# A graph layer's gathers paced over one core: one stage per iteration, and more columns fetched by VectorE and ScalarE

## The chip, the cores and the metric

The kernel runs on one core of a Trainium2 chip. The metric is the device time of one execution in microseconds (us); less is better. "The profile" is one execution recorded by the hardware profiler, "the span" the time from its first to its last instruction. The core's engines work side by side, each through its own queue of instructions in order: TensorE (PE, its weight loads PEld) multiplies matrices, VectorE (DVE) and ScalarE (ACT) work element by element, GpSimd (POOL) issues gathers, SyncE (SP) issues the other transfers. They wait for one another through semaphores.

## The reference

The graph has 12,500 nodes of 64 features (`x`) and 200,000 edges (`src`, `dst`), sorted by `dst`. Each edge has 64 features and a distance. What is computed, with `ssp(v) = softplus(v) - log 2`:

```python
nodes = x[edges].reshape(num_edges, -1)              # 128: x[src], x[dst]
gates = ssp(edge_state @ We1 + be1) @ We2 + be2
gates = gates * (1.0 - sigmoid(5.0 * (edges_distance - 3.5)))
h = ssp(nodes @ Wn1 + bn1) @ Wn2 + bn2
messages = h * gates
message_sum = zeros_like(x).at[edges[:, 1]].add(messages)
new = x + (ssp(message_sum @ Ws1 + bs1) @ Ws2 + bs2)
out = layernorm(x + new)
```

All is float32.

## The kernel before

**Tiling.** The edges are cut into 391 groups of 512 (the last is partly padding). A group is four slots of 128 edges; a slot's rows of `x[src]` come to 128 partitions with one indirect transfer that GpSimd issues (`gather`, L195 to L206): four gathers a group, into a tile `xg` of which eight exist. Since the edges are sorted by target, the 256 edges of half a group reach nodes within a window of 42 rows. So the target side of the first node layer, `x[dst] @ Wn1[64:] + bn1`, is computed once per node in 98 chunks of 128 nodes (`chunk`, `keep_chunk`), stored to a table in HBM, and its window is fetched by SP (`load`, L210 to L226). A one-hot matrix (`onehot`) picks each edge's row, and `scatter` with the same matrix sums the messages.

**A group's way.** `gather` and `load`; `onehot` (VectorE) writes the one-hot columns beside the gathered rows in `xg`; `transposes` (TensorE, L281) bring the four slots to feature-major in PSUM, `xcopy` (ScalarE, L289) copies them to SBUF; `layer1_bias`, `layer1_edge` and `layer1_node` (TensorE) make the 768 pre-activations of edge and node side in a PSUM tile `z`; `exps` and `logs` (ScalarE) and `softplus` (VectorE) the activation; `layer2` (TensorE, L354 and L359) both second layers into a PSUM tile `gh`; `hcut` and `message` (VectorE) multiply h, cutoff and gates; `scatter` (TensorE, L376) sums into a spare part of `z`; `window` (VectorE, L396) adds that to `sums`, which holds the sums of all nodes in SBUF. `z`, `gh` and the transposes' tile `tx` exist twice each.

**The loop.** The order of the work is written out by hand; each engine takes its instructions in that order. Iteration i issues the gathers of group i + 3 and the loads of group i + 5, then on TensorE: biases, `scatter` of group i - 2, `transposes` of i + 1, the edge layer of i + 1, a chunk (or, without one, a matmul whose result nobody reads, `busy`), the node layer of i + 1, another `busy`, `layer2` of i. So within an iteration the node layer waits for `xcopy`, which waits for the transposes just before it; `exps`, `logs` and `softplus` of the same group follow, and `layer2` of group i takes the activation that the iteration before made. A gather waits for its tile: the `scatter` of the group eight before it.

**Columns.** Some slots are not gathered. The kernel holds `x` transposed in SBUF (`xh`, two halves of the nodes on 64 partitions each), and VectorE and ScalarE copy 128 single columns of four bytes each into a tile (`columns`, L259), at addresses that they first load into registers from `columns_at` (`read_columns`, L242, one TENSOR_LOAD an iteration and engine). `choose` keeps the half that holds the node, and `layer1_node` multiplies the result by its own weights. VectorE copies 8 columns an iteration and ScalarE 16, which comes to 70 such slots, in groups that lie apart; those groups gather three slots.

**Node blocks.** When `sums` is complete for a block of 512 nodes (25 blocks), `node_block` runs the output layers and the layer norm in eleven steps, spread over later iterations; the steps of the last block follow the loop. The last twelve iterations run in a closer order (`CLOSE`, `behind_by`), with `scatter` one group behind instead of two.

## Time and profile before

| | |
|---|---|
| runs before | 2359.99, 2363.53, 2370.9 us; median 2363.53 |
| the profiled execution | 2389.88 us, span 2388.1, mean granted TensorE clock 0.981 |
| TensorE busy | 1970.5 us (83% of the span) |
| VectorE, ScalarE busy | 1293.9 (54%), 1511.2 (63%) |
| GpSimd busy | 1417.0 (59%), 1493 gathers |
| columns copied by ScalarE, VectorE | 6016 in 608.7 us, 2944 in 246.5 us |

How to read the lines that follow. A row of the page's groups, or of the view by line, names source line, engine, operation, output and inputs and their shapes, the count, then busy us and mean ns of one, then the idle time of the engine just before them and what ended it. Rows in order of time begin with start and length in us; several like instructions in a row are one row (x8), and a bracket gives the idle time before it with what released it. "issue" means that the profile shows nothing that was waited for. Releasers are inferred from semaphore events, and the ends of matmuls are modelled. A row by windows has the stretch, its length, busy us (instructions) of PE, PEld, DVE, ACT and POOL, the granted clock, the DMA engines' busy share and GB/s. Rows of one line alone give shortest, median and longest ns.

### The profile page before, as it was taken

Reading aid. Unit: us, or ns where it says so; the run is one execution under the profiler, and the core shown is the slowest. Engines: PE = TensorE matmul, PEld = TensorE weight load, DVE = VectorE, ACT = ScalarE, POOL = GpSimd, SP = SyncE. Lnnn points to the kernel's source line nnn. Section 1 sums busy time; section 2 is a strip of 40 time slices with the busy share of each in tenths; the row PEclk is TensorE's granted clock in tenths of the full one; section 3 lists DMA queues with packets and bytes.
Section 4 is the critical chain, followed back from the end, with each engine's and each line's share of the span. In section 5 each row is a group of like instructions: output and inputs, shape, how many; then the busy total and the mean of one; then the engine's idle time right before and its main releaser. Section 6 shows DMA issues by size and latency. Waiting matters only on the chain.

```text
span 2388.1 us, 48209 instructions
## 1 busy us (share of the span) xinstructions
PE 1970.5 (83%) x12897; PEld 1656.7 (69%) x12897; DVE 1293.9 (54%) x5966; ACT 1511.2 (63%) x7412; POOL 1417.0 (59%) x1497
## 2 busy tenths in 40 slices
PE   6788888888888888888888888888888888888877
PEld 4666677767776776677677667766777767777765
DVE  4355555555555555555555555555555555555544
ACT  3466666666666666666666666666666666666653
POOL 5665665666666666666666666665665666666650
PEclk9799999999999999999999999999999999999988
DMA  6332232322222222222222222222222222222220
GB/s 185 85 91 68 56 75 56 77 61 71 54 57 56 53 59 54 57 56 62 53 59 55 57 58 55 59 59 54 58 58 56 59 57 60 63 57 58 59 50 14
DMA packets 159679, 148.63 MB, mean 62 GB/s; under 512 B 40564, under 2 KB 108949, under 8 KB 159274
## 3 DMA queue, kind: packets, MB, share of 16 engines
q1 hardware_dynamic: 111194, 94.97, 14.4%
q0 software_dynamic: 47776, 49.02, 10.8%
q8 instruction: 109, 1.79, 0.3%
q14 instruction: 166, 1.36, 0.2%
q10 hardware_dynamic: 434, 1.50, 0.2%
HBM read 135.70 MB, written 9.62 MB: 61 GB/s over the span
## 4 chain that ended last, share of the span: by engine, by line
PE 80%; issue 13%; ACT 3%; DVE 2%; another core or an unknown queue 1%; DMA 0%; DVEq 0%; ACTq 0%
PE z L308 18%; PE gh L359 13%; PE z L376 10%; PE tx L283 10%; PE gh L354 7%; PE z L301 6%; PE gh L334 4%; PE gh L347 3%; PE z L296 3%; PE z L334 2%; ACT xT L291 2%; PE tx L415 1%; PE tx L446 1%; PE z L311 1%
## 5 line engine op out<-in xcount | busy, mean ns | idle before, releaser
L204 POOL DMA_INDIRECT xg<-in_x,src_i x1493 | 1416.8, 949 | 919.3 <-PE tx L283 488.8
L308 PE MATMUL z<-xT,wns 106*128 106x256 f32 x1564 | 459.7, 412 | 359.9 <-issue 285.9
L291 ACT COPY xT<-tx 106x512 f32<-106x512 f32 x391 | 229.1, 586 | 779.3 <-PE tx L283 751.1
L259 ACT COPY column<-xh 128x4 uint8 x6016 | 608.7, 193 | 0.0
L308 PEld LDWEIGHTS z<-xT,wns 106*128 106x128 f32 x1564 | 267.8, 193 | 452.4 <-issue 337.7
L368 DVE TENSOR_TENSOR h<-gh,cut 128x256 f32<-128x256 f32 x391 | 165.9, 424 | 747.9 <-PE tx L283 632.2
L359 PE MATMUL gh<-consts,s 128*128 128x64 f32 x3128 | 396.0, 270 | 0.0
L359 PEld LDWEIGHTS gh<-consts,s 128*128 128x128 f32 x3128 | 385.0, 194 | 0.1
L325 ACT ACTIVATE u<-u,one 128x768 f32<-128x768 f32 x392 | 365.8, 933 | 13.4 <-ACT u L322 0.5
L330 DVE SCALAR_TENSOR_TENSOR s<-u,z 128x768 f32<-128x768 f32 x392 | 368.7, 941 | 0.4 <-issue 0.4
L322 ACT ACTIVATE u<-z 128x768 f32<-128x768 f32 x392 | 314.7, 803 | 43.4 <-PE z L308 19.0
L396 DVE TENSOR_TENSOR sums<-sums,z 64x42 f32 x778 | 152.4, 196 | 291.3 <-issue 207.4
L376 PEld LDWEIGHTS z<-xg,msg 128*128 128x128 f32 x1556 | 205.0, 192 | 140.6 <-issue 121.3
L376 PE MATMUL z<-xg,msg 128*128 128x84 f32 x1556 | 265.1, 293 | 15.3 <-DVE msg L372 15.3
L259 DVE COPY column<-xh 128x4 uint8 x2944 | 246.5, 219 | 0.4 <-issue 0.4
L354 PE MATMUL gh<-consts,s 128*128 128x128 f32 x1564 | 243.3, 279 | 1.3 <-DVE s L330 0.8
L283 PE MATMUL tx<-consts,xg 128*106 128x128 f32 x1564 | 238.1, 276 | 0.0
L301 PE MATMUL z<-eT,consts 128*128 128x256 f32 x782 | 237.3, 386 | 0.0
L354 PEld LDWEIGHTS gh<-consts,s 128*128 128x128 f32 x1564 | 210.0, 195 | 2.0 <-DVE s L330 1.1
L283 PEld LDWEIGHTS tx<-consts,xg 128*106 128x106 f32 x1564 | 182.5, 142 | 0.9 <-issue 0.9
L372 DVE TENSOR_TENSOR msg<-gh,h 128x256 f32<-128x256 f32 x391 | 165.8, 424 | 13.4
L334 PEld LDWEIGHTS gh<-consts 128*128 128x128 f32 x778 | 149.5, 195 | 20.5 <-issue 0.3
(109 smaller groups left out, 1456.2 us busy)
## 6 DMA issues: line engine op xcount, KB each, us to landing
eT<-in_eT SPq DMA_DIRECT2D x195, 256.0 KB
xg<-in_x,src_i POOLq DMA_INDIRECT x1493
wns<-table SPq DMA_DIRECT2D x782, 21.0 KB
table<-tb SPq DMA_DIRECT2D x14, 448.0 KB
side<-in_sides SPq DMA_DIRECT2D x70, 64.0 KB
y<-in_x SPq DMA_DIRECT2D x24, 128.0 KB
out<-y SPq DMA_DIRECT2D x24, 128.0 KB
xh<-in_xh SPq DMA_DIRECT2D x2, 781.5 KB
```

The costliest lines, as they stand in the source:

```text
L204: behind(note(("gather", g), nc.gpsimd.indirect_dma_start(out=xg[:, k, :D], out_offset=None, in_=x, in_offset=bass.IndirectOffsetOnAxis(ap ...
L259: copy(column_tiles[slot].bitcast(U8)[:, 4 * r : 4 * r + 4], xh[:, bass.ds(column_at[queue][j] - xh_at, 4)])
L283: ins = nc.tensor.transpose(tx[:, k, :], xgs[g][:, k, :DW], ident)
L301: nc.tensor.matmul(zs[g][:, 0, :HE], we1.rearrange("a h d -> a (h d)"), eTs[g], start=False, stop=True, skip_group_check=True)
L308: nc.tensor.matmul(zn, wns[:, g % REST, h, :], xTs[g][:, h], start=True, stop=not chosen, skip_group_check=True)
L322: nc.scalar.activation(us[g][:, part], z_of(g)[:, part], AF.Exp)
L325: nc.scalar.activation(us[g][:, part], us[g][:, part], AF.Ln, bias=one)
L330: nc.vector.scalar_tensor_tensor(ss[g].rearrange("p i t e -> p (i t e)")[:, part], us[g][:, part], BIG, z_of(g)[:, part], OP.min, OP.max)
L334: nc.tensor.matmul(z, we1.rearrange("a h d -> a (h d)"), ident, start=True, stop=True, skip_group_check=True)
L354: nc.tensor.matmul(v[:, 0, t], ss[g][:, 0, t, :], we2, start=False, stop=False, skip_group_check=True)
L359: nc.tensor.matmul(ghs[g][:, 1, 2 * t + h, :], ss[g][:, 1 + h, t, :], wn2, start=False, stop=h == 1 and t == 1, skip_group_check=True)
L376: ins = nc.tensor.matmul(sc, msgs[g][:, 2 * t : 2 * t + 2, :].rearrange("p h f -> p (h f)"), xgs[g][:, 2 * t : 2 * t + 2, D:DW], start=t = ...
```

## The change

*Stages.* Every step of a group has an iteration of its own, by a table of lags: group i is transposed in iteration i, copied out in i + 1, has its first layers in i + 2, exponential and logarithm in i + 3, `softplus` in i + 4, `layer2` in i + 5, message in i + 6, `scatter` in i + 7, `window` in i + 9. On TensorE an iteration runs bias, `scatter`, `layer2`, the edge layer, a chunk or part of a node block, the node layer, the transposes. There is no closer order at the end: the loop goes on until all stages are through.

*`keep`.* A new ScalarE copy brings pre-activations, sums and a node block's or chunk's part (852 or 980 elements) from PSUM to SBUF one iteration after TensorE wrote them; `softplus` and `window` read that copy.

*Gates.* A group's first gather waits for the last `layer2` matmul that the iteration before issued and for the transposes of five groups back; there are twelve `xg` tiles. `load` runs three groups ahead and waits for the same transposes.

*Columns.* VectorE copies 28 and ScalarE 18 columns in an iteration whose group i + 3 gathers four slots, else 20 and 10: 120 slots instead of 70. The addresses of VectorE's columns are loaded in two halves, behind `softplus` and behind `message`; ScalarE's behind the logarithm. `choose` runs one iteration after a slot is whole.

*`busy`.* One stands before the transposes and one before the node layer, both only where group i + 3 gathers four slots, the second only where no chunk and no node block uses the place.

*Node blocks* are cut to parts of 128 columns, one TensorE part an iteration, on a copy of their sums; at most as many iterations as their gaps say. *The start* brings the first 8 groups' indices in a transfer of their own, `x` transposed in 14 pieces, and does part of the preparation inside iterations 1 to 4.

The diff, cut to its core:

```diff
+LAGS = dict(xcopy=1, z=2, exps=3, softplus=4, layer2=5, message=6, sums=7, window=9)
+BUFS = AHEAD + LAGS["sums"] + 2
+GATE = AHEAD + 2
+FETCH = 3
-COLUMNS = (8, 16)
+FEW, MANY = (20, 10), (28, 18)
...
+    def count(queue, i, known):
+        return (FEW if i + AHEAD > known or i + AHEAD in taken else MANY)[queue] if i >= COLUMNS_FROM else 0
...
+    def gather(g):
+        xgs[g] = loads.tile([P, K, P], F32, name="xg", bufs=BUFS)
+        xg, needs, n = xgs[g], [("layer2", g - AHEAD - 1 - LAGS["layer2"]), ("transposes", g - GATE)], 0
...
-        old = ("scatter", g - LOADS - 4)
+        old = ("transposes", g - GATE)
...
     def transposes(g, *needs):
-        tx = tx_tile()[:DW].rearrange("f (k e) -> f k e", k=K)
+        tx = tx_tile()
+        if gathered(g + AHEAD) == K:
+            busy(tx[:, :P])
+        tx = tx[:DW].rearrange("f (k e) -> f k e", k=K)
...
+    def keep(z, n, summed, extra):
+        ends = (0, 3 * HE, 3 * HE + 2 * W, 3 * HE + 2 * W + P)
+        held = [n is not None, summed is not None, bool(extra)]
...
+                nc.scalar.copy(c[:, ends[at] : ends[end]], z.rearrange("p b e -> p (b e)")[:, ends[at] : ends[end]])
...
-        nc.vector.scalar_tensor_tensor(ss[g].rearrange("p i t e -> p (i t e)")[:, part], us[g][:, part], BIG,
-                                       z_of(g)[:, part], OP.min, OP.max)
+        nc.vector.scalar_tensor_tensor(ss[g].rearrange("p i t e -> p (i t e)"), us[g], BIG, cs[g], OP.min, OP.max)
...
+            i = -AHEAD
+            while i <= NG + lag["window"] or blocks:
+                zt = z_tile()
+                n = i - lag["z"]
...
+                at(load, i + FETCH)
+                at(gather, i + AHEAD)
+                at(layer1_bias, n, ("load", n))
+                summed = i - lag["sums"]
+                at(scatter, summed, zt[:, 1, HE : HE + 2 * W])
+                at(layer2_bias, i - lag["layer2"])
+                at(layer2, i - lag["layer2"])
+                at(layer1_edge, n)
...
+                if free and 0 <= n < NG and gathered(i + AHEAD) == K:
+                    busy_before_node(n)
+                at(layer1_node, n)
+                at(transposes, i, ("gather", i), ("onehot", i))
+
+                at(xcopy, i - lag["xcopy"])
+                at(exps, i - lag["exps"])
+                extra = keep(*kept)
+                at(logs, i - lag["exps"])
...
+                at(softplus, i - lag["softplus"])
+                read_columns(i, 0, 0, 2)
+                at(hcut, i - lag["message"])
+                at(message, i - lag["message"])
+                read_columns(i, 0, 1, 2)
+                at(onehot, i + 1)
+                at(window, i - lag["window"])
...
+                read_columns(i, 1)
+                for queue in (1, 0):
+                    if 0 <= i < NG:
+                        columns(i, queue, finish)
```

## Prediction

> **What bounds the kernel now.** I read the page first, then the order of time on each engine in the middle of the run, then the chain of waits, then the start and the end.

> ```profile
> span 2388.1 us, 48209 instructions
> L204 POOL DMA_INDIRECT xg<-in_x,src_i x1493 | 1416.8, 949 | 919.3 <-PE tx L283 488.8
> ```

> No engine is full: GpSimd works 1416.8 of 2388.1 us on 1493 gathers and stands idle 919.3. GpSimd alone, in order of time (start, length, idle time before it):

> ```profile
> 1203.69 0.94 POOL L204 DMA_INDIRECT xg<-in_x,src_i  x1 [1.41 <-PE tx L283]
> 1204.94 0.95 POOL L204 DMA_INDIRECT xg<-in_x,src_i  x1 [0.30 <-issue]
> ...
> 1207.44 0.94 POOL L204 DMA_INDIRECT xg<-in_x,src_i  x1 [0.30 <-issue]
> 1209.87 0.94 POOL L204 DMA_INDIRECT xg<-in_x,src_i  x1 [1.49 <-PE tx L283]
> ...
> 1212.37 0.94 POOL L204 DMA_INDIRECT xg<-in_x,src_i  x1 [0.30 <-issue]
> 1214.66 0.94 POOL L204 DMA_INDIRECT xg<-in_x,src_i  x1 [1.35 <-PE tx L283]
> ```

> A group's gathers form a burst, 1.25 us apart. From burst to burst it takes 6.18 us with four gathers (1203.69 to 1209.87) and 4.79 with three (1209.87 to 1214.66). Between bursts lie 2.43 and 2.29 us instead of 1.25. Why, show the other engines in the same stretch:

> ```profile
> 1205.29 0.66 DVE L259 COPY column<-xh 128x4 uint8 x8
> 1205.79 1.00 PE L359 MATMUL gh<-consts,s 128*128 128x64 f32 x8
> 1207.66 0.60 PE L283 MATMUL tx<-consts,xg 128*106 128x128 f32 x4
> 1209.56 0.42 DVE L368 TENSOR_TENSOR h<-gh,cut 128x256 f32<-128x256 f32 x1 [2.79 <-PE tx L283]
> 1209.69 0.59 ACT L291 COPY xT<-tx 106x512 f32<-106x512 f32 x1 [2.40 <-PE tx L283]
> 1211.70 0.81 ACT L322 ACTIVATE u<-z 128x768 f32<-128x768 f32 x1
> ```

> TensorE ends layer two (L359) at 1206.79 and the transposes (L283) at 1208.26, by its records. Yet VectorE's `hcut`, which needs only L359, starts at 1209.56, ScalarE's `xcopy` at 1209.69, and the next gather, which waits for `scatter` between the two, at 1209.87: all within 0.31 us, and 2.1 us after the last gather of the burst was issued (1207.44). In the three-gather burst the last is issued at 1212.37 and the next burst opens 2.29 us later. At the end, where no gather is left:

> ```profile
> 2346.39 1.00 PE L359 MATMUL gh<-consts,s 128*128 128x64 f32 x8
> 2347.43 0.42 DVE L368 TENSOR_TENSOR h<-gh,cut 128x256 f32<-128x256 f32 x1 [0.26 <-PE gh L359]
> ```

> There `hcut` follows L359 by 0.04 us. So I read: late in a burst TensorE's completions reach nobody until the burst's last gather has landed, some 2.1 us after its issue. Early in a burst they do: L322 starts at 1211.70, right behind the L308 matmuls (below: 1210.33 + 1.13 = 1211.46), 1.8 us into the burst of 1209.87. The chain of waits (start, us, what) shows what TensorE would need by itself:

> ```profile
> 1210.33 1.13 PE z L308 x4
> ...
> 1211.69 0.45 PE gh L354 x4
> 1212.13 0.84 PE gh L359 x8
> 1212.97 0.21 PE z L296
> 1213.18 0.22 PE gh L347
> 1213.40 0.60 PE z L376 x4
> ...
> 1215.10 0.03 issue
> 1215.12 1.13 PE z L308 x4
> ```

> 4.79 us from L308 to L308, of which it waits 0.03: 4.76 of work, against 6.18 a four-gather iteration takes. The bound is the burst, its landing and the wait that opens the next one. From group 11 to group 390 there are 379 such intervals, 70 of them behind three gathers:

> ```profile
> 78.08 0.94 POOL L204 DMA_INDIRECT xg<-in_x,src_i  x1 [3.51 <-remote]
> 2332.80 0.94 POOL L204 DMA_INDIRECT xg<-in_x,src_i  x1 [3.01 <-PE z L376]
> ```

> 309 × 6.18 + 70 × 4.79 = 2245 us; between the two rows lie 2254.7.

> **The change, part by part.** *Fewer gathers.* Written out, the new plan gives 120 groups of three gathers (75 by VectorE, 45 by ScalarE) for 70: fifty intervals shrink by 1.39, 69.5 us. The 50 more side loads (64 KB each) go to SP's queue, none lies in GpSimd's.

> *Engine time for it.* Of the same 102 iterations (us, then busy time of PE, PEld, DVE, ACT, POOL):

> ```profile
> 1000.00:1600.00 600.00, 502.01 (x3352) 423.00 (x3352) 330.39 (x1554) 393.10 (x1966) 368.01 (x389) 1.00 0.24 57
> L259 ACT COPY column<-xh 128x4 uint8 x1628 | 164.7, 193 | 0.0
> L259 DVE COPY column<-xh 128x4 uint8 x808 | 67.0, 221 | 0.0
> L291 ACT COPY xT<-tx 106x512 f32<-106x512 f32 x102 | 59.8, 586 | 199.5 <-PE tx L283 199.5
> L322 ACT ACTIVATE u<-z 128x768 f32<-128x768 f32 x102 | 82.0, 804 | 0.0
> ```

> VectorE: (330.39 - 67.0) / 102 = 2.58 us beside the columns, a column 67.0 / 808 = 0.083; with 28 it has 4.90 us, with 20 4.24. ScalarE: (393.10 - 164.7) / 102 = 2.24, a column 0.101, and `keep`, a new copy of 852 elements out of PSUM in every iteration. Its price lies between 0.80 (L322, 768 elements) and 0.98 (L291's 586 ns scaled by 852/512); I take 0.9. That is 4.96 with 18 columns and 4.15 with 10. All stay under 6.18 and 4.79, so they hide in the idle time that the burst leaves; without that cover a four-gather iteration could not go under 4.96.

> *Address loads.* They run on the sequencers:

> ```profile
> L242 ACTq TENSOR_LOAD <-columns_at x102: 1012/1046/1266, 1000.2 to 1595.5; - x102
> L242 DVEq TENSOR_LOAD <-columns_at x102: 593/614/843, 1004.0 to 1599.3; - x102
> ```

> 16 addresses take 1.046 us and 8 take 0.614, so one more 0.054: two loads of 14 on VectorE 0.94 each, one of 18 on ScalarE 1.15. VectorE's stand behind `softplus` and `message`, ScalarE's behind the logarithm. Bounds: nothing, as now (the copies of 1205.29 follow their neighbour at once), or all of 1.88 us; I take nothing on VectorE and 0.2 on ScalarE.

> *One stage per iteration.* No engine consumes in an iteration what another made in it. What TensorE makes late in a burst is needed one iteration later, so held completions no longer stop it at L308. By itself that shortens nothing while the burst sets the pace. The wasted TensorE matmuls (`busy`) stay two in a four-gather iteration and fall away, 0.44 us, in others.

> *The gate.* A group's first gather now waits for `layer2` of the iteration before and for transposes five groups back, where it waited for a buffer that `scatter` freed. Behind it on GpSimd's queue stand only gathers, needed three iterations later. On SP `load` waits for transposes instead of `scatter`, and is issued three groups ahead for five; behind it wait table, side, y and output transfers, none due in that iteration. `layer2` normally ends late in the burst and is held too, so the gap of 2.43 us stays. But TensorE and ScalarE want only some 5.0 of the 6.18 us and get ahead by up to 1.2 us per burst. Just behind a landing, ScalarE needs `xcopy`, exponential and `keep` (2.3 us), then TensorE L296, L347, L376, L354, L359 (2.32 by the chain's rows): `layer2` ends 4.3 us into the burst. Two or three bursts later it ends before 1.9 us, reaches GpSimd at once, and two bursts run on with one landing: 8.75 + 2.43 = 11.18 instead of 12.36. One such pair in 4.5 groups, 85 of them, would bring 85 × 1.18 = 100 us; none brings 0. I have no row of the new order and take half, 50.

> *Start and end.* Before the first burst that waits for `layer2` (group 9) there are fewer preparations, but deeper stages: between 60 and 85 us for the 78.08 above; I take 70. After the last burst begins the old kernel needs 2388.1 - 2332.8 = 55.3 us. The new one has four full iterations without gathers (4.3 each), two without transposes (3.9), seven with little on TensorE (2) and sixteen steps of the last node block (0.75, a copy, a wait or an activation each), with the rest of the started iteration (2.1) some 53; bounds 43 and 70.

> *The sum.* Of groups 9 to 389, 120 have three gathers and 261 four: 261 × 6.18 + 120 × 4.79 = 2188. With 70, 53 and the 1.8 us by which the profiled execution's 2389.88 exceeds its span: 2313; less 50 gives 2263. The runs' median stands to that profiled execution as 2363.53 to 2389.88, 0.989: **2238 us**. With no pairs 2287, with all 2188; start and end add 15 each way: 2173 to 2305 for this case.

> **The rivals.** *The landings go out of the way.* If completions pass between gathers, four gathers take 5.0 us (GpSimd's own step, about what ScalarE needs) and three 4.4 (TensorE 4.32, VectorE 4.24): 261 × 5.0 + 120 × 4.4 + 125 = 1958, 1936 in runs. For it speak the new slack and gate; against it every burst above. Chance 0.13.

> *Pairs starve the others: slower.* A long burst holds completions longer. GpSimd near the end:

> ```profile
> 2287.97 0.94 POOL L204 DMA_INDIRECT xg<-in_x,src_i  x1 [1.44 <-remote]
> ...
> 2296.72 0.94 POOL L204 DMA_INDIRECT xg<-in_x,src_i  x1 [0.30 <-issue]
> 2301.80 0.94 POOL L204 DMA_INDIRECT xg<-in_x,src_i  x1 [4.14 <-DVE l_s L430]
> ```

> Eight gathers on end took 13.83 us, 1.47 more than 12.36. With 85 pairs at that price the sum is 2313 + 125 = 2438, 2411 in runs. It decides from (2389.9 - 2313) / 85 = 0.9 us a pair. Against it: there TensorE had to make `scatter` anew after the landing, which one stage per iteration avoids. Chance 0.13.

> *The address loads show.* VectorE then has 4.90 + 1.88 = 6.78 us with four gathers, 4.24 + 2 × 0.72 = 5.68 with three: 261 × 6.78 + 120 × 5.68 + 125 = 2576, 2548 in runs. From 6.48 in the four-gather iteration on, that is 1.58 of the 1.88 exposed, it is slower than before. Against it: today's loads lie beside other work at no cost. Chance 0.08.

> *The copies stop the gathers.* If a gather had to wait out VectorE's column copies, the new ones would add 2.32 - 0.66 = 1.66 us to four gathers and 1.0 to three: 2313 + 553 = 2866, 2834 in runs; 0.3 us per four gathers already cancels the gain. Against it: the gather of 1204.94 ran beside the eight copies of 1205.29 and took 0.95 us, as those without did. Chance 0.03. [...]

> **How the numbers follow.** The forecast's own case has 0.63. A measurement here tells 0.5%, 12 us, from no change. Faster by more: 0.63 + 0.13 and 0.02 of the address loads, 0.78. Within: the starving pairs near 0.9 us, 0.04. Slower: their other 0.09, 0.06 of the address loads and the 0.03, 0.18. The range goes from 2080, part of the way to the first rival, to 2410, the starving pairs' price; about 0.1 lies outside on each side.

> **What would show it.** Right: bursts still 1.25 us within, 6.2 and 4.8 from start to start, some of eight gathers followed in 11.2; `hcut` or `xcopy` still grouped behind the landing; 1443 gathers; VectorE and ScalarE each with idle time in four-gather iterations. Wrong: gaps between bursts of 1.25 throughout (first rival), 13 us and more per pair (second), VectorE without idle time and its columns started late behind a load (third), single gathers over 0.95 us or landings later than 2.1 (fourth). Should ScalarE's or VectorE's sum pass 6.2 us, the bound has moved to it and the counting of bursts fails.

## The result and the profile after

| | before | changed |
|---|---|---|
| runs, median | 2366.28 us | 3153.18 us (3146.94 to 3167.03) |
| ratio | 1 | 1.3336, 95% interval 1.3276 to 1.3395 |
| span of the profiled execution | 2388.1 us | 3145.2 us |
| mean granted TensorE clock | 0.981 | 0.761 |

The change makes the kernel a third slower; 2238 us was predicted. (The median before is over four runs here, over three of them ahead of the prediction.) Of all runs below, one of e4 was in a slower state (2476.82 us at a clock of 0.856) and is left out of its median and ratio. The page of the changed kernel, first its summary and chain of waits, then the groups of gathers, columns and `keep`:

```profile
span 3145.2 us, 54782 instructions
PE 2604.0 (83%) x12653; PEld 2123.6 (68%) x12653; DVE 1852.1 (59%) x12870; ACT 1784.1 (57%) x7556; POOL 1446.1 (46%) x1447
...
PEclk8767777787777877886878877778777777777778
...
DVE 46%; DVEq 29%; issue 12%; POOL 5%; PE 4%; DMA 2%; ACT 1%; another core or an unknown queue 1%; ACTq 0%; SPq 0%; POOLq 0%
DVEq L260 26%; DVE column L277 19%; DVE s L373 8%; POOL xg L218 5%; DVE msg L409 4%; DVE h L405 4%; DVE sums L433 4%; DVE xg L298 2%; DMA xg<-in_x,src_i 2%; DVE chosen L292 1%; DVEq L422 1%; DVEq L433 1%; PE gh L395 1%; PE z L334 1%
...
L218 POOL DMA_INDIRECT xg<-in_x,src_i x1443 | 1445.9, 1002 | 1643.7 <-PE gh L395 966.2
L277 DVE COPY column<-xh 128x4 uint8 x9600 | 751.5, 188 | 20.0 <-issue 13.9
L277 ACT COPY column<-xh 128x4 uint8 x5760 | 586.5, 195 | 276.6 <-issue 276.1
...
L361 ACT COPY c<-z 128x852 f32<-128x852 f32 (+4 forms) x402 | 352.4, 877 | 671.5 <-DVE sums L433 454.7
```

VectorE's busy share is only 59%, yet VectorE and its sequencer (DVEq) are 75% of the chain that ended last. The largest line of it, 26%, is L260, the TENSOR_LOAD of the column addresses: time in which VectorE does nothing and counts as idle. The gathers fell to 1443 as planned, and GpSimd now idles 1643.7 us for 919.3, mostly behind TensorE's `layer2`, which in its turn waits for VectorE. VectorE alone, in order of time:

```profile
1207.67 0.33 DVE L298 TENSOR_TENSOR xg<-consts,rel 128x168 f32<-128x168 f32 x1 [3.11 <-issue]
...
1208.35 2.11 DVE L277 COPY column<-xh 128x4 uint8 x28
1210.37 0.94 DVE L373 SCALAR_TENSOR_TENSOR s<-u,c 128x768 f32<-128x768 f32 x1
1211.24 0.41 DVE L405 TENSOR_TENSOR h<-gh,cut 128x256 f32<-128x256 f32 x1
1211.69 0.42 DVE L409 TENSOR_TENSOR msg<-gh,h 128x256 f32<-128x256 f32 x1
1215.08 0.33 DVE L298 TENSOR_TENSOR xg<-consts,rel 128x168 f32<-128x168 f32 x1 [2.97 <-issue]
```

No engine is waited for between `message` and `onehot`, yet VectorE stands 2.97 us. Over the whole run this wait comes to 1030 us (idle time in all, times, longest):

```profile
DVE xg L298 <- issue: 698.0, 271, 3.7
DVE xg L298 <- DMA xg<-in_x,src_i: 331.9, 107, 4.0
```

The second row names a gather, but with that name too `onehot` follows a load: nine in ten of all `onehot` begin 0.09 to 0.26 us behind the end of VectorE's second load. The two loads of this iteration, and ScalarE's, each by its line in a narrow window (min, median and max duration in ns, then first and last start):

```profile
L260 ACTq TENSOR_LOAD <-columns_at x1: 3918/3918/3918, 1208.4 to 1208.4; - x1
L260 DVEq TENSOR_LOAD <-columns_at x1: 1343/1343/1343, 1209.7 to 1209.7; - x1
L260 DVEq TENSOR_LOAD <-columns_at x1: 3289/3289/3289, 1211.7 to 1211.7; - x1
```

Both VectorE loads take 14 addresses: the first 1.34 us, hidden while copies and `softplus` are still in the engine's queue, the second 3.29 us, behind a `message` of 0.42 us that covers next to nothing. ScalarE's load of 18 takes 3.92 us. And it is not always so; ScalarE's loads early, in the middle and late in the run:

```profile
L260 ACTq TENSOR_LOAD <-columns_at x76: 982/1467/1530, 301.9 to 899.3; - x76
L260 ACTq TENSOR_LOAD <-columns_at x103: 2160/3909/4332, 1200.1 to 1996.9; - x103
L260 ACTq TENSOR_LOAD <-columns_at x61: 988/1469/1774, 2399.7 to 2889.4; - x61
```

The addresses lie in `columns_at` in rows of 28 (VectorE) and 18 (ScalarE), a new part of the tile for each 128 iterations. ScalarE's rows start 336, 408 and 480 bytes into it; of these only 408 is no multiple of 16. VectorE's first halves start at 0, 112 and 224 bytes, its second halves 56 or 40 bytes further: the first all multiples of 16, the second none. So theory A: a load is dear by where it starts.

### The profile page after: what moved, and what is told of

It is laid out like the page before. It is cut to its first block, busy times and chain, and to the rows that moved or that the text cites. A ratio compares the mean times of both kernels' runs of the same rounds, so it can differ in the third digit from the quotient of the medians.

```text
span 3145.2 us, 54782 instructions
## 1 busy us (share of the span) xinstructions
PE 2604.0 (83%) x12653; PEld 2123.6 (68%) x12653; DVE 1852.1 (59%) x12870; ACT 1784.1 (57%) x7556; POOL 1446.1 (46%) x1447
## 4 chain that ended last, share of the span: by engine, by line
DVE 46%; DVEq 29%; issue 12%; POOL 5%; PE 4%; DMA 2%; ACT 1%; another core or an unknown queue 1%; ACTq 0%; SPq 0%; POOLq 0%
DVEq L260 26%; DVE column L277 19%; DVE s L373 8%; POOL xg L218 5%; DVE msg L409 4%; DVE h L405 4%; DVE sums L433 4%; DVE xg L298 2%; DMA xg<-in_x,src_i 2%; DVE chosen L292 1%; DVEq L422 1%; DVEq L433 1%; PE gh L395 1%; PE z L334 1%
## 5 line engine op out<-in xcount | busy, mean ns | idle before, releaser
L218 POOL DMA_INDIRECT xg<-in_x,src_i x1443 | 1445.9, 1002 | 1643.7 <-PE gh L395 966.2
L277 DVE COPY column<-xh 128x4 uint8 x9600 | 751.5, 188 | 20.0 <-issue 13.9
L277 ACT COPY column<-xh 128x4 uint8 x5760 | 586.5, 195 | 276.6 <-issue 276.1
L298 DVE TENSOR_TENSOR xg<-consts,rel 128x168 f32<-128x168 f32 x391 | 130.6, 334 | 1029.9 <-issue 698.0
L361 ACT COPY c<-z 128x852 f32<-128x852 f32 (+4 forms) x402 | 352.4, 877 | 671.5 <-DVE sums L433 454.7
L334 PE MATMUL z<-xT,wns 106*128 106x256 f32 x1564 | 568.0, 495 | 6.4 <-issue 6.4
L395 PE MATMUL gh<-consts,s 128*128 128x64 f32 x3128 | 532.0, 330 | 1.8 <-issue 1.7
L395 PEld LDWEIGHTS gh<-consts,s 128*128 128x128 f32 x3128 | 526.2, 254 | 2.0 <-issue 2.0
L373 DVE SCALAR_TENSOR_TENSOR s<-u,c 128x768 f32<-128x768 f32 x391 | 367.2, 939 | 22.9 <-ACT u L348 10.2
L390 PE MATMUL gh<-consts,s 128*128 128x128 f32 x1564 | 354.5, 362 | 0.0
L327 PE MATMUL z<-eT,consts 128*128 128x256 f32 x782 | 354.4, 546 | 0.0
L390 PEld LDWEIGHTS gh<-consts,s 128*128 128x128 f32 x1564 | 263.6, 240 | 116.1 <-issue 115.8
L433 DVE TENSOR_TENSOR sums<-sums,c 64x42 f32 x782 | 153.5, 196 | 68.5 <-issue 63.2
```

The costliest lines, as they stand in the source:

```text
L218: ins = note(("gather", g), nc.gpsimd.indirect_dma_start(out=xg[:, k, :D], out_offset=None, in_=x, in_offset=bass.IndirectOffsetOnAxis(ap= ...
L277: copy(column_tiles[slot].bitcast(U8)[:, 4 * r : 4 * r + 4], xh[:, bass.ds(column_at[queue][j] - xh_at, 4)])
L327: nc.tensor.matmul(zs[g][:, 0, :HE], we1.rearrange("a h d -> a (h d)"), eTs[g], start=False, stop=True, skip_group_check=True)
L334: nc.tensor.matmul(zn, wns[:, g % REST, h, :], xTs[g][:, h], start=True, stop=not chosen, skip_group_check=True)
L361: nc.scalar.copy(c[:, ends[at] : ends[end]], z.rearrange("p b e -> p (b e)")[:, ends[at] : ends[end]])
L373: nc.vector.scalar_tensor_tensor(ss[g].rearrange("p i t e -> p (i t e)"), us[g], BIG, cs[g], OP.min, OP.max)
```

## The experiments

Each set of runs has the kernel before beside it on the same chip, and the sets came from chips that differ: the kernel before took 2363 us in the first, 1994 us in the second, third and fifth, and 2394 us in the fourth. So only ratios are compared across sets.

### First set: is it where a load starts?

**e1_aligned.** VectorE's loads are split at a multiple of four addresses, and ScalarE's rows lie 20 addresses apart.

```diff
+ROW = (28, 20)
...
-        first, last = (count * j // parts for j in (part, part + 1))
+        first, last = (count if j == parts else count * j // parts // 4 * 4 for j in (part, part + 1))
...
-            row, column = ..., queue * columns_of[0] + (i - COLUMNS_FROM) // P * MANY[queue]
+            row, column = ..., queue * columns_of[0] + (i - COLUMNS_FROM) // P * ROW[queue]
```

> Theory A (where a load starts): in the trace of the changed kernel a load of column addresses that starts at a multiple of 16 bytes takes 1.33 to 1.35 us for 14 addresses and 1.48 for 18, one that starts 8 bytes past such a multiple takes 3.27 for 14, 2.36 for 10 and 4.0 for 18, and VectorE stands some 2.9 us of each iteration behind its second load. Here only the places change: VectorE's 28 addresses are split 12 and 16, its 20 split 8 and 12, and ScalarE's rows are 20 addresses apart, so all start at a multiple of 16 bytes. A expects every load at or under 1.6 us, some 2 us less per iteration for VectorE, its idle time before the one-hot comparison down from about 3.0 to under 1.2 us, and 2300 to 2550 us. Theory B (the granted clock of TensorE, 0.76, sets the pace whatever VectorE does): shorter loads, clock still under 0.85, over 2950 us. Theory C (the order of one stage per iteration and its gate set the pace): 3050 to 3200 us, VectorE idle elsewhere instead.

**e2_addresses_once.** On top of that, the addresses of the first iteration with columns are kept for all later ones: later loads are left out, every copy is still made, of the wrong columns.

```diff
+        if i > COLUMNS_FROM and count:
+            column_at[queue] = first_at[queue]
...
-        if first < last:
+        elif first < last:
```

> As the kernel with aligned loads, but the addresses are loaded in the first iteration with columns only and used again in all later ones, so the output misses the right rows; every copy is still made. A expects VectorE near 5 us per iteration without any wait behind a load, and 2230 to 2380 us, a little below the kernel with aligned loads, the difference being what aligned loads still cost. B and C expect no change to the changed kernel, 3050 us or more.

**e3_before_off16.** The kernel before, its addresses two columns further in the tile.

```diff
-            columns_at[p : p + 1, q : q + count], engines=...
+            columns_at[p : p + 1, q + 2 : q + 2 + count], engines=...
```

> The kernel before with its column addresses laid 8 bytes further in their tile, nothing else changed. A expects loads of 8 addresses at about 1.9 us for 0.61 and of 16 at about 3.7 for 1.05, and, since ScalarE's work with that would be 3.9 + 2.6 = 6.5 us for an iteration that takes 6.2, some slowing: 2380 to 2600 us. A rival A2 (the long loads come of the new order: two loads close together, more live registers, or queued copies) expects 0.61 and 1.05 as before and the time of the kernel before, 2366 us.

**e4_old_columns.** `FEW, MANY = (8, 16), (8, 16)` in the changed kernel.

> The changed kernel with the column numbers of the kernel before, 8 and 16 in every iteration: the order of one stage per iteration, the gate and the split loads stay. Its loads, 4 and 4 and 16, all start at multiples of 16 bytes. A expects loads of at most 1.1 us, bursts of 6.2 and 4.8 us as before and 2300 to 2420 us. C expects the order itself to be slow: 2900 us or more, with the same idle time on GpSimd. B expects a clock under 0.85 here too, and a time over 2600 us.

| | median us | ratio, interval | clock |
|---|---|---|---|
| e1_aligned | 2509.47 | 1.0653 (1.0582 to 1.0724) | 0.87 |
| e2_addresses_once | 2392.05 | 1.0155 (1.0104 to 1.0206) | 0.883 |
| e3_before_off16 | 2742.36 | 1.162 (1.158 to 1.166) | 0.894 |
| e4_old_columns | 2435.5 | 1.0319 (1.0263 to 1.0374) | 0.877 |

The loads by line between 1000 and 1600 us, first of the kernel with aligned loads, then of the kernel before with shifted addresses, with the line shares of its chain:

```profile
L261 DVEq TENSOR_LOAD <-columns_at x193: 595/875/1154, 999.9 to 1600.0; - x193
L261 ACTq TENSOR_LOAD <-columns_at x96: 982/1469/1727, 1003.1 to 1595.6; - x96
```

```profile
L242 ACTq TENSOR_LOAD <-columns_at x89: 3409/3497/3639, 1000.1 to 1594.4; - x89
L242 DVEq TENSOR_LOAD <-columns_at x89: 1840/1899/2139, 1001.4 to 1596.8; - x89
...
ACTq L242 20%; PE z L308 10%; ACT column L259 10%; ACT u L325 7%; PE gh L359 7%; ACT u L322 6%; ACT xT L291 5%; PE z L376 5%; PE gh L354 4%; PE tx L283 3%; PE z L301 2%; PE gh L334 2%; PE gh L347 2%; PE z L296 1%
```

Eight bytes are all that e3 changes, and its loads of 8 and 16 take 1.90 and 3.50 us for 0.61 and 1.05; the new order, the split and the registers in use (A2) have no part in that. Its time lies above the 2380 to 2600 us expected: ScalarE's load alone is 20% of the chain. With the starts mended the changed kernel is 6.5% slower than the one before, for 33.4%. VectorE's stretch in it, next to the one above:

```profile
1206.16 0.42 DVE L410 TENSOR_TENSOR msg<-gh,h 128x256 f32<-128x256 f32 x1
1207.39 0.33 DVE L299 TENSOR_TENSOR xg<-consts,rel 128x168 f32<-128x168 f32 x1 [0.81 <-issue]
...
1208.08 2.08 DVE L278 COPY column<-xh 128x4 uint8 x28
...
1211.40 0.42 DVE L410 TENSOR_TENSOR msg<-gh,h 128x256 f32<-128x256 f32 x1
1212.37 0.34 DVE L299 TENSOR_TENSOR xg<-consts,rel 128x168 f32<-128x168 f32 x1 [0.55 <-issue]
```

The wait before `onehot` falls from 2.97 to 0.55 and 0.81 us. Without later loads (e2) another 117 us go: that is what aligned loads still cost. B (the clock alone) and C (the order alone), which expected 2950 us or more of e1 and e2, are out. But e1 and e2 stay above the kernel before, and e4 too, whose loads are short (0.35 us for 4); e2 and e4 also lie 12 and 16 us above what A allowed. A explains most of the loss, not all of the distance to the forecast.

### Second and third set: what is left?

The chain of the kernel with addresses loaded once, by engine, then TensorE in it, in order of time, then windows of the same stretch (length, busy time of PE, PEld, DVE, ACT, POOL with counts, clock, DMA share, GB/s):

```profile
PE 73%; DVE 9%; ACT 7%; issue 5%; another core or an unknown queue 3%; DMA 1%; SPq 0%; DVEq 0%; POOL 0%; ACTq 0%
```

```profile
1043.21 0.29 PE L315 MATMUL tx<-consts,xg 128*106 128x128 f32 x1 [0.47 <-issue]
1045.30 0.37 PE L327 MATMUL z<-ones,be 3*128 3x256 bf16 x1 [1.80 <-ACT c L366]
```

```profile
1036.00:1041.00 5.00, 5.00 (x35) 4.21 (x34) 2.65 (x12) 0.52 (x6) 4.05 (x4) 1.00 0.12 26
1041.00:1045.00 4.00, 1.27 (x7) 0.64 (x6) 2.82 (x31) 1.81 (x3) 1.97 (x3) 0.98 0.24 60
1045.00:1060.00 15.00, 14.70 (x53) 11.94 (x53) 9.92 (x67) 11.46 (x58) 6.99 (x7) 0.50 0.25 67
1060.00:1065.00 5.00, 5.00 (x28) 3.91 (x27) 3.78 (x35) 2.64 (x4) 3.81 (x4) 0.81 0.12 30
```

TensorE works 1.27 of the 4 us from 1041, and then stands at half clock for 15 us, though busy all the while. So theory D, the clock, against E (VectorE's remaining loads) and F (the order itself).

e5, e6 and e8 are built on e1, with its aligned loads. **e5_more_busy** has three wasted matmuls for one at both places and one for none; **e6_keep_first** puts `exps` and `keep` ahead of `xcopy`; **e8_both** does both; **e7_before_no_busy** takes the wasted matmuls out of the kernel before (the body of `busy` is `pass`).

> The kernel with aligned loads (2509 us, clock 0.87) and more wasted matmuls: three for one at both places of a four-gather iteration, one for none in the others, at 0.22 us each 0.9 and 0.4 us more for TensorE per iteration. Theory D (what is left is TensorE's clock: after an idle stretch the trace shows it at half for whole multiples of 3.41 us, in which an iteration takes 9 us): the clock goes above 0.95, the half-speed time falls from 632 us to under 200, and the time to 2330 to 2430 us. Theory E (what is left is VectorE's remaining load time and the waits it makes; the low clock is a companion): the clock may rise, the time stays within 40 us of 2509 or grows by TensorE's extra 0.9 us where that is on the path.

> The kernel with aligned loads, and ScalarE's exponential and its copy of the last z (line of keep) put ahead of its copy of the transposes, which is told of late in a burst; TensorE needs the two to have a z buffer free. In a trace with half-speed stretches one began with TensorE waiting 1.80 us for keep just behind such a wait. Theory D expects TensorE's waits on keep to fall away, fewer half-speed stretches (77 before, under 50 here), clock above 0.92, and 2380 to 2460 us. Theory E expects no change beyond 30 us of 2509.

> The kernel before without its wasted matmuls (0.22 us each, two in most iterations), nothing else changed; the output is as before. It shows in the old order whether the clock hangs on TensorE's idle time. Theory D expects more idle time per window, half-speed stretches well above the 12 and 84 us of the kernel before (over 40 and over 250 us), a clock under 0.92, and a time 2 to 12% over 2363 us though the work is less. Theory E expects the clock to fall at most a little and the time to stay within 1%, since the bursts of gathers set the pace there.

> Aligned loads, more wasted matmuls and keep ahead of the copy of the transposes, all together. Theory D expects a clock above 0.96 and 2270 to 2380 us, near or below the kernel before. Theory E expects 2450 us or more.

**e9_after_again** is the changed kernel as it is. **e10_once_busy** and **e12_old_columns_busy** are e2 and e4 with three wasted matmuls in four-gather and two in other iterations, **e11_before_16** is e7 with `COLUMNS = (16, 16)`.

> The changed kernel as it is, beside the kernel before on the chip of this set; the kernel before took 2363 us on one chip and 1994 on another, where GpSimd's gathers ran 1.25 us apart without a pause. Theory A (VectorE's misaligned loads and its columns are the chain that sets the pace) expects 3080 to 3180 us whichever chip it is, for nothing in that chain hangs on when gathers land, so a ratio of 1.33 or of 1.55 to 1.6. If the landings mattered beside the loads, the time would fall with that of the kernel before, to 2660 us where that takes 1994.

> The kernel that loads its addresses once (its output misses the right rows; every copy is made), with a wasted matmul more per four-gather iteration, 0.2 us, and two for none in the others, 0.4 us. In that kernel TensorE was 73% of the chain at a mean clock of 0.88. Theory D (its half-speed stretches are what is left) expects a clock above 0.94, and a time 1.5 to 5% under 2392 us where the kernel before takes 2363, that is a ratio of 0.96 to 1.00. Theory F (the order of one stage per iteration costs by its waits, whatever the clock) expects the ratio to stay at 1.01 to 1.03.

> The kernel before without its wasted matmuls, and with 16 columns by VectorE for 8: 94 groups of three gathers for 70, each load 16 addresses from a multiple of 64 bytes. Each further three-gather group is expected to save one gather, 1.25 to 1.39 us, 30 to 33 us in all. On a chip without the pause at the landing: 0.95 to 0.965 of the kernel before, where the version without wasted matmuls alone had 0.969. On a chip with the pause: theory D expects the missing matmuls to cost clock, 1.00 to 1.10; otherwise 0.98 to 0.99.

> The changed kernel with the old column numbers, 8 and 16, which had a ratio of 1.032 to the kernel before and a clock of 0.88, with the same further wasted matmuls as the kernel above. Theory D expects a clock above 0.94 and a ratio of 0.985 to 1.01 where the kernel before takes 2363 us. Theory F expects 1.03 as before or more.

| before takes 1994 us | median us | ratio, interval | clock |
|---|---|---|---|
| e5_more_busy | 2305.77 | 1.156 (1.1528 to 1.1592) | 0.976 |
| e6_keep_first | 2324.5 | 1.1656 (1.1619 to 1.1692) | 0.901 |
| e7_before_no_busy | 1934.76 | 0.969 (0.9664 to 0.9717) | 0.992 |
| e8_both | 2310.44 | 1.1575 (1.1545 to 1.1606) | 0.969 |
| e9_after_again | 3050.92 | 1.5293 (1.5263 to 1.5322) | 0.768 |
| e10_once_busy | 2075.84 | 1.0403 (1.0382 to 1.0424) | 0.992 |
| e11_before_16 | 1949.4 | 0.9776 (0.9753 to 0.9798) | 0.99 |
| e12_old_columns_busy | 2076.04 | 1.0408 (1.039 to 1.0427) | 0.992 |

On these two chips the pause at the landing, on which the forecast rests, does not show. The kernel before was only timed there; its version without wasted matmuls was traced (e7):

```profile
1201.29 0.95 POOL L204 DMA_INDIRECT xg<-in_x,src_i  x1 [0.30 <-issue]
1201.39 0.60 PE L283 MATMUL tx<-consts,xg 128*106 128x128 f32 x4
1202.03 0.59 ACT L291 COPY xT<-tx 106x512 f32<-106x512 f32 x1 [0.79 <-PE tx L283]
1202.55 1.01 POOL L204 DMA_INDIRECT xg<-in_x,src_i  x1 [0.30 <-issue]
```

`xcopy` starts 0.04 us after the transposes end (1201.99), with a gather just issued; 1428 of its 1492 steps from gather to gather are between 1.2 and 1.3 us in its trace. So these sets do not answer for the first chip, and the absolute times that were expected for that chip say nothing here. What they do show: the changed kernel takes 3051 us even where nothing holds the completions (e9; 3080 to 3180 was expected, so some 3% of its 3153 may hang on the landings). Its loads and columns are the pace, on both kinds of chip. Its loads there, between 1000 and 1600 us:

```profile
L260 DVEq TENSOR_LOAD <-columns_at x158: 1066/1944/3374, 1001.0 to 1597.2; - x158
L260 ACTq TENSOR_LOAD <-columns_at x79: 1024/3903/4255, 999.5 to 1594.6; - x79
```

e5, e6 and e8 lie within 1% of one another, though their clocks go from 0.90 to 0.98. First the chain of e6 by engine, then e10 from 1000 to 1600 us (columns as above):

```profile
DVE 63%; DVEq 13%; PE 10%; issue 7%; POOL 3%; DMA 1%; ACT 1%; ACTq 0%; POOLq 0%
```

```profile
1000.00:1600.00 600.00, 600.00 (x4016) 506.17 (x4017) 542.82 (x3893) 517.17 (x2294) 418.83 (x426) 1.00 0.29 67
```

VectorE and its loads, aligned as they are, are three quarters of e6's chain: theory E, on such a chip. Without loads (e10) TensorE is busy all 600 us at full clock, and e12, with 8 and 16 columns for 28 and 18, takes the same 2076 us: there the matmuls are the bound, and not the waits that theory F names. In e12 304 of TensorE's 2043 busy us are wasted matmuls; the changed order without them was not run on such a chip, so what the order costs there stays open. e7 fell against D's expectation: without wasted matmuls the clock stayed at 0.992, with TensorE busy 93% of e7's span, and the kernel is 3.1% faster than the one before. Sixteen columns for VectorE (e11) came to 0.978 for the 0.95 to 0.965 expected, and did not better it.

### Fourth set: the clock or the order, on a chip with the pause

The changed kernel with the old columns and no, two and three wasted matmuls (**e13**, **e14**, **e15**; e14 is e4 again, e15 is e12 again); and **e16**, the aligned kernel with `FEW, MANY = (16, 8), (16, 16)` and no wasted matmul.

> The changed kernel with the old column numbers (8 and 16, aligned loads) and without any wasted matmul; TensorE's work per iteration falls by 0.44 us against the same kernel with its two. Where the kernel before takes 1994 us, theory F expects 0.94 to 0.98 of it, since TensorE was 97% of the chain there with more of them (ratio 1.041). Where it takes 2363 us, theory D expects a clock under 0.85 and a ratio of 1.04 to 1.10, theory F 1.00 to 1.03.

> The changed kernel with the old column numbers and its two wasted matmuls in four-gather iterations, the middle of three. Where the kernel before takes 2363 us it was 1.032. Where it takes 1994 us, theory F expects 0.98 to 1.02, between the ones without and with more; theory D expects it above both if its clock is under 0.92.

> The changed kernel with the old column numbers and more wasted matmuls (three with four gathers, two with three). Where the kernel before takes 1994 us: 1.041 as measured. Where it takes 2363 us: theory D a clock above 0.94 and 0.985 to 1.01, theory F 1.03 or more.

> The order of the changed kernel with 16 and 8 columns in an iteration that gathers three and 16 and 16 in one that gathers four, all loads of 8 or 16 addresses from multiples of 32 bytes, and no wasted matmul: 88 groups of three gathers for 70. VectorE then has about 2.6 + 1.3 + 0.7 = 4.6 us per iteration, TensorE 4.3. Where the kernel before takes 1994 us, 0.92 to 0.97; where it takes 2363 us, 0.97 to 1.00 by theory F, above 1.03 by theory D.

| before takes 2394 us | median us | ratio, interval | clock |
|---|---|---|---|
| e13_old_columns_no_busy | 2501.79 | 1.0418 (1.0361 to 1.0476) | 0.816 |
| e14_old_columns_again | 2469.06 | 1.0303 (1.0274 to 1.0332) | 0.873 |
| e15_old_columns_busy_again | 2450.68 | 1.0231 (1.0213 to 1.0249) | 0.901 |
| e16_16_no_busy | 2481.15 | 1.037 (1.0329 to 1.041) | 0.828 |

The more work is wasted, the faster: 51 us from e13 to e15, as D has it. e13 and e16, with no wasted matmul and clocks of 0.82 and 0.83, are above 1.03 as D expects and F does not. But for e15 D expected a clock above 0.94 and 0.985 to 1.01, F 1.03 or more: its 1.0231 is neither, and its clock of 0.901 is under what D asked for. How the gathers run in e15 shows in its trace, GpSimd, ScalarE, VectorE and one step of TensorE in order of time:

```profile
1131.17 0.96 DVE L373 SCALAR_TENSOR_TENSOR s<-u,c 128x768 f32<-128x768 f32 x1 [6.74 <-remote]
1131.34 1.61 POOL L218 DMA_INDIRECT xg<-in_x,src_i  x1 [2.08 <-remote]
...
1134.87 0.96 DVE L373 SCALAR_TENSOR_TENSOR s<-u,c 128x768 f32<-128x768 f32 x1 [0.39 <-issue]
...
1138.65 0.60 PE L310 MATMUL tx<-consts,xg 128*106 128x128 f32 x4
1139.58 0.94 POOL L218 DMA_INDIRECT xg<-in_x,src_i  x1 [0.30 <-issue]
1140.83 0.95 POOL L218 DMA_INDIRECT xg<-in_x,src_i  x1 [0.31 <-issue]
1143.25 0.59 ACT L318 COPY xT<-tx 106x512 f32<-106x512 f32 x1 [7.58 <-PE gh L395]
1143.67 0.95 POOL L218 DMA_INDIRECT xg<-in_x,src_i  x1 [1.89 <-remote]
...
1146.28 0.96 DVE L373 SCALAR_TENSOR_TENSOR s<-u,c 128x768 f32<-128x768 f32 x1 [8.06 <-issue]
```

Eight gathers run from 1131.34 to 1140.83 in one burst. ScalarE waits 7.58 us for transposes that ended at 1139.25 by their record, and starts 2.42 us after the last gather was issued; VectorE's `softplus` behind it stood 8.06 us. If a burst is what GpSimd issues with less than 0.8 us of idle time between, 4% of the gathers of the kernel before stand in bursts of more than four, and 69% in e15.

That such a merged burst starves the others looks like the rest of the loss (theory G, below), but the traces do not bear it out. From its first gather to the next burst a burst of eight takes 12.49 us in e15 (the mean of 71) and 12.32 in e2 (of 20); two of four apart take 2 × 6.18 = 12.36. The loss is elsewhere. Bursts of four that stand alone take 6.19 us in e15 and 6.16 in e2 where the mean clock was above 0.95 meanwhile, 7.23 and 6.94 where it was lower (39 of 96 in e15, 69 of 150 in e2). Against 6.18 and 4.79 us, e15's bursts are 90 us over in sum, 66 of that in single bursts with the lower clock; in e13, without wasted matmuls, it is 135 and 131. Nor does the clock fall more often in merged bursts: 35 of 55 falls in e15 lie in them, and they take 67% of the time. Whether the low clock made those bursts long, or their waiting made the clock low, the sums alone do not show; that wasted matmuls halve the excess speaks for the first.

One more thing costs GpSimd time. The first gather above takes 1.61 us for 0.95: it begins while `softplus` runs (1131.17 to 1132.13) and ends 0.82 us behind it. In the kernel before a `softplus` of the same shape does a gather no harm:

```profile
1711.56 0.94 DVE L330 SCALAR_TENSOR_TENSOR s<-u,z 128x768 f32<-128x768 f32 x1
1711.77 0.94 POOL L204 DMA_INDIRECT xg<-in_x,src_i  x1 [1.30 <-DVE msg L372]
```

Of the gathers that begin while `softplus` runs, 3 of 366 take over 1.05 us in the kernel before, 161 of 224 in the changed kernel and 259 of 301 in e15, nearly all ending 0.81 to 0.82 us behind `softplus`. What differs in the instruction is that `softplus` now reads `c`, which `keep` put in SBUF, where it read `z` in PSUM. In sum the gathers of e15 take 167 us more than 0.946 each, those of the kernel before 4. The new order with a `softplus` that reads PSUM was not run, so what this costs in time is not known.

### Fifth set: bursts kept apart

**e17_paced** and **e18_16_paced** set `PACE = "landing"`: a group's first gather also waits for the landing of the last one of the group before; e17 is e15 with that, e18 the aligned kernel with e16's columns and its own wasted matmuls.

> The changed kernel with the old column numbers and more wasted matmuls (ratio 1.023 with the pause, 1.041 without it), and each group's first gather now also waits until the last gather of the group before has landed, so no two bursts can run together. Theory G (bursts that run together starve ScalarE and VectorE, then TensorE) expects, where the kernel before takes about 2370 us, no burst over four gathers, no wait of ScalarE for the transposes over 3 us, a clock above 0.95, 6.0 to 6.2 us per four-gather group and a ratio of 0.98 to 1.005. If the order costs for another reason, 1.02 or more. Where the kernel before takes 1994 us the wait is new there and costs about 0.9 us per group: 1.10 to 1.15.

> The order of the changed kernel with 16 and 8, or 16 and 16 columns, aligned loads, its own two wasted matmuls in four-gather iterations, 88 groups of three gathers for 70, and the same wait for the landing of the group before. Theory G expects 0.965 to 1.00 where the kernel before takes about 2370 us: 18 more three-gather groups at 1.39 us take some 25 us, 0.01, off the kernel above, and fewer wasted matmuls may give a part back by the clock. If the order costs for another reason, 1.02 or more. Where the kernel before takes 1994 us: 1.09 to 1.14.

They ran where the kernel before takes 1994 us, and took 2805.79 us (1.4079, 1.4053 to 1.4105) and 2796.19 (1.4019, 1.3962 to 1.4077), far above the 1.09 to 1.15 expected: between two groups 3.3 to 3.7 us lie from issue to issue in the stretch from 1199 to 1218 of e17's trace, where 2.1 had been reckoned for the landing, and ScalarE and VectorE waited behind it (ScalarE's `xcopy` 207 us for the transposes in the 600 us from 1000 on). Without the pause nothing needs keeping apart, so this set does not test theory G on the first chip; against it stand the traces of the fourth set alone.

## Why the prediction was wrong

**The step that failed is the price and the cover of the address loads.** From loads of 16 in 1.046 and of 8 in 0.614 us it took 0.054 for each further address, hence 0.94 for 14 and 1.15 for 18, called that hidden on VectorE, and bounded it by 1.88. The medians of all loads in the traces, by number and by the first one's offset in the tile:

| addresses | offset a multiple of 16 bytes | 8 bytes past one |
|---|---|---|
| 4 | 0.35 us | |
| 8 | 0.61 | 1.90 |
| 10 | 1.09 (VectorE), 1.01 (ScalarE) | 2.36 (VectorE), 2.24 (ScalarE) |
| 12 | 0.87 | |
| 14 | 1.35 | 3.27 |
| 16 | 1.04 (ScalarE), 1.12 (VectorE) | 3.56 |
| 18 | 1.49 | 4.01 |

Worked out from it: on VectorE four more aligned addresses cost 0.25 to 0.26 us; a pair left over 0.45 to 0.48 (10 against 8, 14 against 12, 18 against 16), and misaligned loads 0.22 to 0.24 for every address, where an aligned 16 in 1.046 us comes to 0.065 each. Starts 4 or 12 bytes past a multiple of 16 were not measured. Both loads the prediction took its line from were aligned and had no pair over, so no line through them could hold for two times 14.

The cover failed as well: of the two loads only the one behind `softplus` was hidden (1209.7 to 1211.08, with `softplus` busy to 1211.31). Behind `message` 0.42 us of work cover a load of 3.29, and 2.97 stay. So the bound "all of 1.88" was no bound.

**The rival "the address loads show" is what happened**, with its mechanism and its point of decision: it had 6.78 us for a four-gather iteration and decides from 6.48; the iteration above took 7.41 (1207.67 to 1215.08 from `onehot` to `onehot`). Its 2548 us were 605 too low, first of all for the price of the second load: it had 261 × 1.88 + 120 × 1.44 = 663 us for both loads, and the wait before `onehot` alone is 1030. TensorE, left idle by engines that waited for VectorE, fell to a clock of 0.76, but is only 4% of the chain; the remaining 240 us or so were not taken apart. Its point of 6.48 was too high: it leaves iterations with three gathers at 4.79 us, though as large a share of their 1.44 exposed puts them at 5.45; with both counted the point is 6.25.

**The engine times were right.** A column took 751.5 / 9600 = 0.078 us on VectorE and 586.5 / 5760 = 0.102 on ScalarE (0.083 and 0.101 predicted), `keep` 0.88 (0.9). GpSimd issued 1443 gathers. The rival by which copies stop the gathers is ruled out at its price (2834 us): e2 makes all 15,360 copies and takes 2392, and in the changed kernel the 470 gathers that begin in a VectorE column copy take 0.947 us in the median. But its sign, single gathers over 0.95 us, came: 183 of the 1443 take over 1.05, 161 of them begun while `softplus` ran. That `softplus` from SBUF costs the gathers nothing was assumed without a row.

**Start and end were near.** In e2, group 9's first gather starts at 58.4 us (70 predicted, 60 to 85 as bounds), and from the last group's first gather at 2326.7 to the end it is 58.1 (53). (In the range worked out from these bounds, 2287 + 15 is 2302, not 2305, which decides nothing.)

**With the loads gone the forecast would still have been wrong.** e2 is its world without address loads, and took 2392 us for 2238. In the prediction's terms, from a group's first gather to the next group's it took 6.35 us with four gathers and 5.10 with three, in the mean, for 6.18 and 4.79: 261 × 6.35 + 120 × 5.10 = 2269, where the sum had 2188 less 50. Two steps are behind that. "Two bursts run on with one landing" was booked as a gain of 50 us. Bursts did merge, but their eight gathers took 9.69 us to issue in e2 and 9.83 in e15 for 8.75, since some began while `softplus` ran, and from the last issue to the next burst it took 2.63 and 2.67 for 2.43: 12.32 and 12.49 us for the 11.18 reckoned, which is no gain, nor the 13.83 of the rival "pairs starve the others". And the clock does not appear in the sum at all: of the 81 us above 2188, all lie in single bursts with a lowered clock (87 us over; the merged ones are 5 under). From e13 to e15 wasted work won back 51 us by it. Whether the clock alone made those bursts long was not settled.

**The bound before was read rightly for that chip only.** Completions held until a landing stand in its rows (`xcopy` 2.25 us behind the last gather's issue) and again in the fourth set (2.42 us in e15), but not on the chips of the second, third and fifth: in e7's trace `xcopy` follows the transposes by 0.04 us, and the kernel before takes 1994 us in all three sets.

## What to carry to other kernels

Look at every single load of registers in the trace, with its offset and count: start it at a multiple of 16 bytes, take addresses by fours (in this case a start 8 bytes past was 2.2 to 3.4 times the price, and a pair left over cost 0.45 to 0.48 us), and never interpolate a price between two that share an alignment. A load on a sequencer is hidden by what its engine still has queued at that moment, not by the instruction it is written behind in general (here 1.34 us behind `softplus` were hidden, and of 3.29 behind a `message` of 0.42 us 2.97 stayed); price it against that one's length. When an engine's busy share is low and its sequencer stands in the chain (here VectorE with 59% busy and its sequencer with 29% of the chain), the wait is its own.
